# A GNN's first edge loop: two VectorE operands moved to PSUM, one-hots turned by TensorE, one score product instead of three, steps staggered

## Chip, cores, metric

One NeuronCore of a Trainium2 chip runs the whole program. The metric is the device time of one execution in microseconds (us), lower is better. The executions of one kernel are fast, that is, within 1.5% of the fastest execution of the same kernel in the same call. In the profile's lines PE is TensorE, PEld its loading of weights, DVE VectorE, ACT ScalarE and POOL GpSimd; SBUF and PSUM are the two on-chip memories in which the programs put the operands.

## The reference

Four layers work on N = 4096 nodes with D = 512 features and E = 65536 edges, sorted by destination. Only layer 0, a graph attention with H = 8 heads of F = 64, is concerned:

```python
def _L0_gnn_ref(x, edge_index, W, a):          # adj holds the edges and the diagonal
    h = jnp.einsum('nc,hcf->hnf', x, W)
    s_src = jnp.einsum('hnf,hf->hn', h, a[:, :F, 0])
    s_dst = jnp.einsum('hnf,hf->hn', h, a[:, F:, 0])
    e = s_src[:, :, None] + s_dst[:, None, :]
    e = jnp.where(e > 0, e, ALPHA * e)
    e = jnp.where(adj[None, :, :], e, NEG_INF)
    att = jax.nn.softmax(e, axis=-1)
    out = jnp.einsum('hij,hjf->hif', att, h)
    ...
x = x + _L0_gnn_ref(relu(layernorm(x)), edge_index, L0_gnn_W, L0_gnn_a)
# layers 1 to 3: other edge sums and dense products, unchanged by this case
```

## The kernel before

The edges are cut into tiles of 128, and eight tiles make a group; layer 0 has 68 groups. For each tile POOL issues one indirect gather: 128 rows of 2080 bytes, the node's 512 features and its eight score parts. The other part of a score belongs to the edge's own block of 128 nodes. It is fetched by a product of a turned one-hot matrix (`oh_t`, node by edge) with the block's node parts, which are kept as three bf16 pieces. VectorE weighs heads 0 to 5 of the rows, ScalarE heads 6 and 7; TensorE sums the rows into their nodes with the one-hot matrix (`oh`, edge by node); VectorE adds each pair's sum to `acc` ("keeps" it).

```python
def one_hots(pool, loc, t0, n):
    oh = pool.tile([P, n, P], F32, name="oh")
    nc.vector.tensor_tensor(oh, row_i.unsqueeze(1).to_broadcast([P, n, P]),          # L454
                            loc[:, t0:t0 + n].unsqueeze(2).to_broadcast([P, n, P]), op=OP.is_equal)
    return oh

# inside attend(): ep, eps are pools of two buffers (SBUF, PSUM)
def fetch(g):
    rows = ep.tile([P, GT, DA], F32, name="rows", bufs=4)
    for j in range(GT):
        gather(rows[:, j, :D + H], htab, s_dst[:, at(g) + j:at(g) + j + 1])          # L459, POOL
    return rows

def source_parts(g, places):          # places: the edges' node numbers, broadcast by a DMA
    oh_t = ep.tile([P, GT * P], BF16, name="oh_t")
    nc.vector.tensor_scalar(oh_t, places, col_i, None, op0=OP.is_equal)              # L703
    e_ps = eps.tile([P, GT, 2, H], F32, name="e_ps")
    ...                                # of[:, j // 2] = the block's three node parts, ScalarE
    for j in range(GT):
        for k in range(3):
            nc.tensor.matmul(e_ps[:, j]..., oh_t[:, j * P:(j + 1) * P],
                             of[:, j // 2, k, :], start=k == 0, stop=k == 2)         # L711
    return e_ps

def scores(rows, e_ps):
    u = ep.tile([P, GT, H], F32, name="u")
    nc.vector.tensor_add(u, e_ps[:, :, 0, :], rows[:, :, D:D + H])                   # L717
    ...                                # leaky relu, minus the bound, exp on ScalarE

def weights(g, rows, u):
    nc.vector.tensor_mul(rows[:, :, D:D + H], u, s_new[...]...)
    return one_hots(ep, s_loc, at(g), GT)

def weigh(j, rows):
    two = rows[:, j:j + 2]
    ...                                # heads 6 and 7 on ScalarE
    g = two[:, :, :VH * F].rearrange("p t (h f) -> p t h f", h=VH)
    nc.vector.tensor_mul(g, g, two[:, :, D:D + VH].unsqueeze(3).to_broadcast([P, 2, VH, F]))   # L739

# add_up: eight matmuls of a pair of tiles (L745); keep: acc += the pair's sum (L752)
for g in range(-3, groups):            # `if now(...)` guards cut
    rows[g + 3] = fetch(g + 3)
    places[g + 2] = fetch_places(g + 2)
    e_ps = source_parts(g + 1, places.pop(g + 1))
    ps = None
    for j in range(0, GT, 2):
        weigh(j, rows[g])
        if ps is not None:
            keep(g, j - 2, ps)
        ps = add_up(g, j, rows[g], done[g])
        if j == 2:
            u = scores(rows[g + 1], e_ps)
    done[g + 1] = weights(g + 1, rows[g + 1], u)
    keep(g, GT - 2, ps)
```

## Time and profile before

| | before |
|---|---|
| time, median of 4 runs (range) | 6489.0 us (6481.7 to 6496.5) |
| span of the profiled run | 6491.6 us |
| layer 0 edge loop, first gather to last keep | 277.9 to 1049.4 us: 771.5 us |
| distance of successive groups' scores, mean | 11.09 us |

The page's busy shares for the whole program do not speak of this loop: TensorE's come mostly from layer 2's dense products (2887 of its 5701 us lie between 2250 and 5230 us).

```profile
PE 5700.9 (88%) x18462; PEld 2779.8 (43%) x18462; DVE 4140.9 (64%) x7147; ACT 2940.7 (45%) x3977; POOL 3264.9 (50%) x3326
```

How to read the lines that follow in this document. A group of instructions has: line, engine, operation, tiles, shapes, count | busy us, mean ns of one | idle us just before them, and what ended it. A wait has: the engine, tile and line that waited, what released it, then us in all, number of waits, longest one. A timeline line has: start, duration, instruction, count, and in brackets the idle time before it. The loop itself is read in a stretch of steady state, as the prediction does.

### The profile page before, as it was taken

To read this page: it belongs to the slowest core of one execution; us is meant where nothing else is said; L and a number is where in the kernel's file an instruction comes from. 1 tells how busy PE (TensorE), PEld (TensorE's weight loads), DVE (VectorE), ACT (ScalarE), POOL (GpSimd) and SP (SyncE) were. 2 spreads that over 40 slices of the span, in tenths; PEclk is the share of its full clock that TensorE was granted. 3 is DMA by queue.
4 is the path that set the end of the run, shared out by engine and by line. 5 is a ranking of instruction groups with operands and counts; after the bars stand their busy time and mean duration, and the time that the engine had idled before them with its cause. 6 is when DMAs were issued, how large, how long until landed. Compare 5 with 4: busy or idle time off the path is not lost. (4 is left out here: it accounts for less than half of the span.)

```text
span 6491.6 us, 65768 instructions
## 1 busy us (share of the span) xinstructions
PE 5700.9 (88%) x18462; PEld 2779.8 (43%) x18462; DVE 4140.9 (64%) x7147; ACT 2940.7 (45%) x3977; POOL 3264.9 (50%) x3326
## 2 busy tenths in 40 slices
PE   6677787888779799999999999999999879978877
PEld 4366664322224344444444444444444456532222
DVE  7577778455534267766766766766776635556666
ACT  3244444300001277777777777777777633310000
POOL 1277772377760365555555555555555200017776
PEclk9899999999999899999999999999999999989999
DMA  8777775566774333333333333333333121127777
GB/s 226 181 215 219 216 218 172 164 201 201 195 215 177 130 115 100 98 105 101 99 102 103 99 100 105 99 98 106 100 99 104 52 81 62 62 93 209 222 243 221
DMA packets 400530, 926.42 MB, mean 143 GB/s; under 512 B 136695, under 2 KB 136695, under 8 KB 400151
## 3 DMA queue, kind: packets, MB, share of 16 engines
q0 software_dynamic: 230976, 721.66, 38.3%
q1 hardware_dynamic: 169174, 200.39, 9.8%
q8 instruction: 155, 2.54, 0.2%
q14 instruction: 225, 1.84, 0.1%
HBM read 818.71 MB, written 103.11 MB: 142 GB/s over the span
## 5 line engine op out<-in xcount | busy, mean ns | idle before, releaser
L448 PE MATMUL m_ps<-w_sb,h_t 128*128 128x512 f32 x4224 | 1906.0, 599 | 31.2 <-ACT h_t L969 31.2
L813 PE MATMUL sum_ps<-g,oh 128*128 128x512 f32 x2144 | 1133.7, 633 | 245.9 <-DMA g<-ztab,d_src 94.6
L448 PEld LDWEIGHTS m_ps<-w_sb,h_t 128*128 128x128 f32 x4224 | 771.2, 190 | 983.8 <-issue 791.3
L459 POOL DMA_INDIRECT qg<-qtab,eg x528 | 505.2, 957 | 990.2 <-ACT h_t L969 844.9
L459 POOL DMA_INDIRECT g<-ztab,d_src x528 | 514.0, 974 | 864.7 <-DMA x_end<-x 704.1
L469 DVE TENSOR_TENSOR acc<-acc,sum_ps 128x512 f32 x800 | 549.9, 687 | 543.8 <-PE sum_ps L813 517.4
L813 PEld LDWEIGHTS sum_ps<-g,oh 128*128 128x128 f32 x2144 | 340.7, 191 | 1026.6 <-DVE acc L469 356.5
L459 POOL DMA_INDIRECT g<-ytab,s_dst x544 | 535.5, 984 | 357.2 <-DMA ytab<-acc 187.9
L926 POOL DMA_INDIRECT eg<-aug,d_eid x528 | 568.9, 1077 | 244.1 <-issue 135.3
L459 POOL DMA_INDIRECT rows<-htab,s_dst x544 | 584.8, 1075 | 204.9 <-issue 139.3
L969 ACT COPY h_t<-tr_ps 128x512 f32<-128x512 f32 x528 | 283.7, 589 | 777.5 <-PE tr_ps L967 777.5
L745 PE MATMUL sum_ps<-rows,oh 128*128 128x261 f32 x2176 | 548.3, 408 | 62.1 <-PE sum_ps L745 37.0
L459 POOL DMA_INDIRECT pg<-ptab,eg x528 | 508.0, 962 | 160.9 <-issue 160.6
L745 PEld LDWEIGHTS sum_ps<-rows,oh 128*128 128x128 f32 x2176 | 425.4, 201 | 163.8 <-PE sum_ps L745 60.1
L979 PE MATMUL small_ps<-z,oh 128*128 128x512 f32 x1056 | 477.9, 595 | 8.4 <-DVE z L1039 8.4
L1018 DVE TENSOR_TENSOR z<-m_ps,b_bc 128x512 f32<-128x512 f32 x132 | 91.3, 692 | 467.4 <-PE m_ps L448 467.4
L469 DVE TENSOR_TENSOR acc<-acc,small_ps 128x512 f32 x528 | 360.8, 683 | 31.9 <-PE small_ps L979 4.4
L1192 ACT ACTIVATE t_end<-acc,dis 128x512 f32<-128x512 f32 x32 | 23.0, 721 | 663.7 <-DVE acc L469 663.7
L1004 DVE TENSOR_TENSOR z<-m_ps,b_bc 128x512 f32<-128x512 f32 x132 | 91.3, 692 | 352.9 <-PE m_ps L448 352.9
L1039 DVE TENSOR_TENSOR z<-z,t 128x1024 f32<-128x1024 f32 x264 | 310.3, 1217 | 8.2 <-ACTq L474 4.8
L979 PEld LDWEIGHTS small_ps<-z,oh 128*128 128x128 f32 x1056 | 201.5, 191 | 263.7 <-issue 221.9
L967 PEld LDWEIGHTS tr_ps<-ident,pg 128*128 128x128 f32 x2112 | 247.7, 141 | 150.8 <-issue 119.7
(252 smaller groups left out, 8389.0 us busy)
## 6 DMA issues: line engine op xcount, KB each, us to landing
aug<-row SPq DMA_DIRECT2D x32, 560.0 KB, 4.1
places<-loc_rows SPq DMA_DIRECT2D x68, 256.0 KB, 4.0
xt<-in_x_dram SPq DMA_DIRECT2D x16, 1024.0 KB, 6.5
row<-in_edge_attr_dram SPq DMA_DIRECT2D x32, 512.0 KB, 6.7
x<-xt SPq DMA_DIRECT2D x16, 1024.0 KB, 4.3
rows<-htab,s_dst POOLq DMA_INDIRECT x544, 3.9
g<-ytab,s_dst POOLq DMA_INDIRECT x544, 3.7
eg<-aug,d_eid POOLq DMA_INDIRECT x528, 2.7
```

Of the source, the lines that this page charges most:

```text
L448: nc.tensor.matmul(ps, h_t[:, k, :], w_sb[:, k0 + k, :], start=start and k == 0, stop=stop and k == KC - 1)
L459: nc.gpsimd.indirect_dma_start(out=dst_ap, out_offset=None, in_=table, in_offset=bass.IndirectOffsetOnAxis(ap=idx, axis=0))
L469: nc.vector.tensor_add(into, into, ps)
L745: nc.tensor.matmul(ps[:, c, :HW], oh[:, j + k, :], rows[:, j + k, c * HW:(c + 1) * HW], start=k == 0, stop=k == 1)
L813: nc.tensor.matmul(ps, oh[:, j + k, :], g[:, j + k, :], start=k == 0, stop=k == pair - 1)
L926: nc.gpsimd.indirect_dma_start(out=eg[:, j // 2, (j % 2) * HALF:(j % 2 + 1) * HALF], out_offset=None, in_=aug.rearrange("e c -> (e c)").un ...
L967: nc.tensor.transpose(h_ps[:, k, :], h[:, j, k * P:(k + 1) * P], ident)
L969: nc.scalar.copy(h_t, h_ps)
L979: nc.tensor.matmul(ps, oh, m, start=True, stop=True)
L1004: nc.vector.tensor_add(zz[:, 0, :], ps, b2_bc)
L1018: nc.vector.tensor_add(zz[:, 1, :], ps, b2_bc)
L1039: nc.vector.tensor_mul(mz[:, j:j + 2], mz[:, j:j + 2], t[:, j:j + 2])
```

## The change

Its intent: POOL's gathers take longer where they meet the weighing multiplies or the one-hots of the kernel before, VectorE instructions with two operands in SBUF (up to 1.73 us beside L739 and 1.95 beside L454, 0.947 in the median). So the weights that the multiply reads, and the node numbers that the one-hots compare with, go to PSUM. The room that this leaves is to be used by a shorter cycle of VectorE and TensorE: the turned one-hots come from TensorE and ScalarE instead of a VectorE compare of data that a DMA brings, the three parts of a score come from one product of 48 columns and are summed on VectorE, and the steps of neighbouring groups are interleaved. The core of the diff (removal of `loc_rows`, `col_i` and pieces that only change names are cut):

```diff
-    def one_hots(pool, loc, t0, n):
+    def one_hots(pool, loc, t0, n, bufs=None, ids=None):
-        nc.vector.tensor_tensor(oh, row_i.unsqueeze(1).to_broadcast([P, n, P]),
+        nc.vector.tensor_tensor(oh, (row_i if ids is None else ids).unsqueeze(1).to_broadcast([P, n, P]),
...
+            both_ps = kept.tile([P, P + 2 * GT * H], F32, name="both_ps")      # PSUM
+            ids_ps = both_ps[:, :P]
+            w_ps = both_ps[:, P:].rearrange("p (k t h) -> p k t h", k=2, t=GT)
+            nc.scalar.copy(ids_ps, row_i)
...
+            def turn(oh):                              # two t_ps tiles of four transposes each
+                        nc.tensor.transpose(t_ps[:, k, :], oh[:, j + k, :], ident)
-                nc.vector.tensor_scalar(oh_t, places, col_i, None, op0=OP.is_equal)
+                    nc.scalar.copy(oh_t[:, 4 * j:4 * j + 4, :], t_ps)
...
-                    for k in range(3):
-                        nc.tensor.matmul(e_ps[:, j]..., oh_t[:, j * P:(j + 1) * P],
-                                         of[:, j // 2, k, :], start=k == 0, stop=k == 2)
+                    nc.tensor.matmul(e_ps[:, j].rearrange("p k c -> p (k c)"), oh_t[:, j, :],
+                                     of[:, j // 2].rearrange("p k c -> p (k c)"), start=True, stop=True)
...
+                nc.vector.reduce_sum(near, e_ps.rearrange("p t k c -> p t c k"), axis=AX.X)
...
-                nc.vector.tensor_mul(rows[:, :, D:D + H], u, s_new...)
+                w = w_ps[:, g % 2]
+                nc.vector.tensor_mul(w, u, s_new...)
+                nc.scalar.copy(rows[:, :, D:D + H], w)
...
-                nc.vector.tensor_mul(g, g, two[:, :, D:D + VH].unsqueeze(3).to_broadcast([P, 2, VH, F]))
+                nc.vector.tensor_mul(part, part,
+                                     w_ps[:, g % 2, j:j + 2, :VH].unsqueeze(3).to_broadcast([P, 2, VH, F]))
...
+                rows[g + 3] = fetch(g + 3)             # the new order of a step, guards cut
+                made = turn(ohs[g + 1])
+                weigh(g, 0, rows[g]); sums[0] = add_up(g, 0, ...); weigh(g, 2, rows[g])
+                keep(g - 1, 6, sums.pop(6))
+                parts = turned(g + 1, made)
+                sums[2] = add_up(g, 2, ...); weigh(g, 4, rows[g]); keep(g, 0, sums.pop(0))
+                ohs[g + 2] = one_hots(ep, s_loc, at(g + 2), GT, 3, ids_ps)
+                e_ps = source_parts(*parts)
+                sums[4] = add_up(g, 4, ...)
+                u = scores(rows[g + 1], e_ps)
+                weigh(g, 6, rows[g]); keep(g, 2, sums.pop(2)); sums[6] = add_up(g, 6, ...)
+                weights(g + 1, rows[g + 1], u)
+                keep(g, 4, sums.pop(4))
```

More of the change, by code (lines that the diff above doesn't have):

```diff
@@ L88 @@
                    allow_small_or_imprecise_dtypes=True)
-    col_i = const.tile([P, 1], F32, name="col_i")
-    nc.gpsimd.iota(col_i, pattern=[[0, 1]], base=0, channel_multiplier=1,
-                   allow_small_or_imprecise_dtypes=True)
     acc = keep_pool.tile([P, NB, DA], F32, name="acc")
@@ L118 @@
     aug = dram.tile([E + 1, EA], F32, name="aug")
-    loc_rows = dram.tile([G * P, P], BF16, name="loc_rows")
     x1 = dram.tile([N, D], F32, name="x1")
@@ L315, in by_order @@
         placed(s_loc, loc)
-        low_p = pool.tile([P, G, P], BF16, name="low_p")
-        nc.vector.tensor_copy(low_p, loc)
-        nc.sync.dma_start(loc_rows.rearrange("(g p) c -> p g c", p=P), low_p)
         new = pool.tile([P, G, P], F32, name="new")
@@ L449, in product @@
                              start=start and k == 0, stop=stop and k == KC - 1)
-    def one_hots(pool, loc, t0, n):
-        oh = pool.tile([P, n, P], F32, name="oh")
-        nc.vector.tensor_tensor(oh, row_i.unsqueeze(1).to_broadcast([P, n, P]),
+    def one_hots(pool, loc, t0, n, bufs=None, ids=None):
+        oh = pool.tile([P, n, P], F32, name="oh", bufs=bufs)
+        nc.vector.tensor_tensor(oh, (row_i if ids is None else ids).unsqueeze(1).to_broadcast([P, n, P]),
                                 loc[:, t0:t0 + n].unsqueeze(2).to_broadcast([P, n, P]), op=OP.is_equal)
@@ L682, in run @@
             eps = ctx.enter_context(tc.tile_pool(name="edge_ps", bufs=2, space=PSUM))
+            kept = ctx.enter_context(tc.tile_pool(name="edge_keep", bufs=1, space=PSUM))
+            both_ps = kept.tile([P, P + 2 * GT * H], F32, name="both_ps")
+            ids_ps = both_ps[:, :P]
+            w_ps = both_ps[:, P:].rearrange("p (k t h) -> p k t h", k=2, t=GT)
+            nc.scalar.copy(ids_ps, row_i)
             groups = (last - first) // GT
@@ L693, in fetch, with turned @@
                 return rows
-            def fetch_places(g):
-                places = ep.tile([P, GT * P], BF16, name="places", bufs=3)
-                nc.sync.dma_start(places, loc_rows[at(g):at(g) + GT].rearrange("t c -> (t c)").partition_broadcast(P))
-                return places
-            def source_parts(g, places):
-                oh_t = ep.tile([P, GT * P], BF16, name="oh_t")
-                nc.vector.tensor_scalar(oh_t, places, col_i, None, op0=OP.is_equal)
-                e_ps = eps.tile([P, GT, 2, H], F32, name="e_ps")
+            def turn(oh):
+                made = []
+                for j in range(0, GT, 4):
+                    t_ps = eps.tile([P, 4, P], F32, name="t_ps")
+                    for k in range(4):
+                        nc.tensor.transpose(t_ps[:, k, :], oh[:, j + k, :], ident)
+                    made.append(t_ps)
+                return made
+            def turned(g, made):
+                oh_t = ep.tile([P, GT, P], BF16, name="oh_t")
+                for j, t_ps in enumerate(made):
+                    nc.scalar.copy(oh_t[:, 4 * j:4 * j + 4, :], t_ps)
                 of = ep.tile([P, GT // 2, 3, 2 * H], BF16, name="of")
@@ L708, in source_parts @@
                     nc.scalar.copy(of[:, j // 2], node3[:, ds(b, 1)].rearrange("p b k c -> p (b k) c"))
+                return oh_t, of
+            def source_parts(oh_t, of):
+                e_ps = eps.tile([P, GT, 3, 2 * H], F32, name="e_ps", bufs=1)
                 for j in range(GT):
-                    for k in range(3):
-                        nc.tensor.matmul(e_ps[:, j].rearrange("p c h -> p (c h)"), oh_t[:, j * P:(j + 1) * P],
-                                         of[:, j // 2, k, :], start=k == 0, stop=k == 2)
+                    nc.tensor.matmul(e_ps[:, j].rearrange("p k c -> p (k c)"), oh_t[:, j, :],
+                                     of[:, j // 2].rearrange("p k c -> p (k c)"), start=True, stop=True)
                 return e_ps
             def scores(rows, e_ps):
+                near = ep.tile([P, GT, 2 * H], F32, name="near")
+                nc.vector.reduce_sum(near, e_ps.rearrange("p t k c -> p t c k"), axis=AX.X)
                 u = ep.tile([P, GT, H], F32, name="u")
-                nc.vector.tensor_add(u, e_ps[:, :, 0, :], rows[:, :, D:D + H])
+                nc.vector.tensor_add(u, near[:, :, :H], rows[:, :, D:D + H])
                 nc.vector.scalar_tensor_tensor(u, u, 0.2, u, op0=OP.mult, op1=OP.max)
-                nc.vector.tensor_sub(u, u, e_ps[:, :, 1, :])
+                nc.vector.tensor_sub(u, u, near[:, :, H:])
                 nc.vector.tensor_scalar(u, u, SAFE_RANGE + 10.0, None, op0=OP.min)
@@ L726, in weights, with weigh_last @@
             def weights(g, rows, u):
-                nc.vector.tensor_mul(rows[:, :, D:D + H], u,
-                                     s_new[:, at(g):at(g) + GT].unsqueeze(2).to_broadcast([P, GT, H]))
-                return one_hots(ep, s_loc, at(g), GT)
-            def weigh(j, rows):
+                w = w_ps[:, g % 2]
+                nc.vector.tensor_mul(w, u, s_new[:, at(g):at(g) + GT].unsqueeze(2).to_broadcast([P, GT, H]))
+                nc.scalar.copy(rows[:, :, D:D + H], w)
+            def weigh_last(j, rows):
                 two = rows[:, j:j + 2]
@@ L737, in weigh @@
                                              scale=two[:, k, D + h:D + h + 1])
-                g = two[:, :, :VH * F].rearrange("p t (h f) -> p t h f", h=VH)
-                nc.vector.tensor_mul(g, g, two[:, :, D:D + VH].unsqueeze(3).to_broadcast([P, 2, VH, F]))
+            def weigh(g, j, rows):
+                part = rows[:, j:j + 2, :VH * F].rearrange("p t (h f) -> p t h f", h=VH)
+                nc.vector.tensor_mul(part, part,
+                                     w_ps[:, g % 2, j:j + 2, :VH].unsqueeze(3).to_broadcast([P, 2, VH, F]))
             def add_up(g, j, rows, oh):
@@ L752, in keep @@
                 nc.vector.tensor_add(into, into, ps[:, :, :HW])
-            rows, places, done = {}, {}, {}
-            for g in range(-3, groups):
+            rows, ohs, sums = {}, {}, {}
+            for g in range(-3, groups + 1):
                 now = lambda k: 0 <= k < groups
@@ L758, in run @@
                     rows[g + 3] = fetch(g + 3)
+                if now(g + 1):
+                    made = turn(ohs[g + 1])
+                if now(g):
+                    weigh(g, 0, rows[g])
+                    sums[0] = add_up(g, 0, rows[g], ohs[g])
+                    weigh_last(2, rows[g])
+                    weigh(g, 2, rows[g])
+                if now(g - 1):
+                    keep(g - 1, 6, sums.pop(6))
+                    del rows[g - 1], ohs[g - 1]
+                if now(g + 1):
+                    parts = turned(g + 1, made)
+                if now(g):
+                    sums[2] = add_up(g, 2, rows[g], ohs[g])
+                    weigh_last(4, rows[g])
+                    weigh(g, 4, rows[g])
+                    keep(g, 0, sums.pop(0))
                 if now(g + 2):
-                    places[g + 2] = fetch_places(g + 2)
+                    ohs[g + 2] = one_hots(ep, s_loc, at(g + 2), GT, 3, ids_ps)
                 if now(g + 1):
-                    e_ps = source_parts(g + 1, places.pop(g + 1))
-                ps = None
-                for j in range(0, GT, 2):
-                    if now(g):
-                        weigh(j, rows[g])
-                        if ps is not None:
-                            keep(g, j - 2, ps)
-                        ps = add_up(g, j, rows[g], done[g])
-                    if j == 2 and now(g + 1):
-                        u = scores(rows[g + 1], e_ps)
+                    e_ps = source_parts(*parts)
+                if now(g):
+                    sums[4] = add_up(g, 4, rows[g], ohs[g])
                 if now(g + 1):
-                    done[g + 1] = weights(g + 1, rows[g + 1], u)
+                    u = scores(rows[g + 1], e_ps)
                 if now(g):
-                    keep(g, GT - 2, ps)
-                    del rows[g], done[g]
+                    weigh_last(6, rows[g])
+                    weigh(g, 6, rows[g])
+                    keep(g, 2, sums.pop(2))
+                    sums[6] = add_up(g, 6, rows[g], ohs[g])
+                if now(g + 1):
+                    weights(g + 1, rows[g + 1], u)
+                    weigh_last(0, rows[g + 1])
+                if now(g):
+                    keep(g, 4, sums.pop(4))
         run()
```

## The prediction

> **What bounds the kernel now.** I read first the page, to find the stage, then one stretch of the steady edge loop of layer 0 (320 to 1000 us) as a table of busy times, as groups and as waits, then one group of eight tiles in order of time. The change touches this loop alone: its first gather starts at 277.9 us and its last sum is kept at 1049.4 us, 771 us of 6490, 12%. The stretch (columns: length, then busy us of PE, PEld, DVE, ACT, POOL, granted clock, DMA share, GB/s) and the page's row of the gathers:
>
> ```profile
> 320.00:1000.00 680.00, 540.39 (x3432) 424.41 (x3432) 532.09 (x921) 300.67 (x1342) 530.21 (x492) 0.95 0.77 217
> ```
>
> ```profile
> L459 POOL DMA_INDIRECT rows<-htab,s_dst x544 | 584.8, 1075 | 204.9 <-issue 139.3 <-ACT of L708 39.4 <-PE sum_ps L745 10.7
> ```
>
> PE, DVE and POOL each look busy for about 79%, so busy share names no bound. The gaps do. The waits of the stretch (us in total, times, longest):
>
> ```profile
> DVE acc L752 <- PE sum_ps L745: 136.9, 128, 3.0
> POOL rows L459 <- issue: 124.6, 409, 0.3
> ...
> PE e_ps L711 <- DVE oh_t L703: 85.9, 61, 1.5
> ...
> DVE u L717 <- DMA rows<-htab,s_dst: 3.7, 8, 0.8
> ```
>
> POOL's gaps are 0.30 us each and never longer, in front of every gather: that is the price of issuing, not a wait. 492 gathers of 1.079 us and their gaps fill 680 us, so **POOL never stands still**, and eight gathers set a pace of 11.07 us per group. The scores of successive groups start 11.11 us apart on average: the same. But VectorE and TensorE, waiting on each other (136.9 and 85.9 us above), are hardly faster. Undisturbed groups start 10.7 us apart; 24 of 67 take over 11.3 us, up to 12.4, and 23 of those meet one of the stretches of 3.4 us in which the granted clock is half, some 44 us apart (mean clock 0.95). So two loops of nearly equal length run side by side, and both must shrink for the stage to shrink.
>
> Why a gather takes 1.08 us when its median is 0.947 is seen where a group is laid out in time (start, us):
>
> ```profile
> 728.04 0.95 POOL L459 DMA_INDIRECT rows<-htab,s_dst  x1 [0.30 <-issue]
> 729.29 0.96 POOL L459 DMA_INDIRECT rows<-htab,s_dst  x1 [0.30 <-PE sum_ps L745]
> 730.56 1.62 POOL L459 DMA_INDIRECT rows<-htab,s_dst  x1 [0.30 <-issue]
> 732.49 0.95 POOL L459 DMA_INDIRECT rows<-htab,s_dst  x1 [0.30 <-issue]
> ```
>
> ```profile
> 729.97 0.54 DVE L703 TENSOR_SCALAR oh_t<-places,col_i 128x1024 bf16<-128x1024 bf16 x1
> 730.42 1.81 DVE L739 TENSOR_TENSOR rows<-rows 128x768 f32<-128x768 f32 x2
> 734.38 0.70 DVE L752 TENSOR_TENSOR acc<-acc,sum_ps 128x522 f32 x1 [2.14 <-PE sum_ps L745]
> ```
>
> The gather that meets the two weighing multiplies (L739, both inputs in SBUF) takes 1.62 us; those beside the sum from PSUM (L752) take 0.95. Counted over the loop, 135 of 544 gathers exceed 1.0 us, and the excess over 0.947 is 69 us, 62 us of it beside L739 and 7 beside the one-hots (L454) and L703.
>
> [...] The trace shows stretches of 3.4 us at 0.5, though TensorE never idles that long here (longest wait 1.7 us). In the next layer's loop, at 339 us busy of 400 (85%), the clock is 1.00. [...] at 512 elements an add from PSUM (L1150) takes 692 ns and one from SBUF (L1139) 685. So I charge nothing for moving an operand to PSUM.
>
> **The change part by part**, per group of eight tiles.
>
> *POOL.* The multiplies read their weights, and the one-hots their node numbers, from PSUM: one SBUF input each. The bf16 compare L703 goes. What remains with two SBUF inputs are short score steps (0.22 to 0.25 us each). The floor is 8 x (0.947 + 0.303) = 10.00 us; I allow 0.05 for the short steps: 10.05 against 11.07.
>
> *VectorE*, in intervals from start to start in the trace: four multiplies 4 x 0.87 = 3.48, four sums 4 x 0.61 = 2.44, one-hots 1.14, score steps 0.25 + 0.26 + 0.25 + 0.11 = 0.87, weight product 0.17. Removed: L703, 0.46. Added: the sum of a score's three parts, 384 elements; a reduction over 512 takes 0.668 us (L838), so 0.54, and 0.56 with the wait of the next step. Sum 8.7 us: not the bound.
>
> *TensorE.* The score products go from 24 matmuls to 8 of 48 columns, 0.76 to about 0.3 us. Added are eight transposes; layer 2 has them (eight in 1.04 us, one lasting 0.273, so 0.11 from start to start):
>
> ```profile
> 3000.45 1.04 PE L967 MATMUL tr_ps<-ident,pg 128*128 128x128 f32 x8
> ```
>
> Eight cost 0.87 us. Each of the four pair sums is eight matmuls 0.22 us apart, 1.76 us. Total 0.87 + 7.04 + 0.3 = 8.2 us.
>
> *ScalarE.* Added: two evictions of 128x512 (0.589 us each, L969) and one copy of weights (0.2). 300.67 / 61.3 = 4.9 us per group becomes 6.3: not the bound.
>
> *Order of steps.* The order of the changed program puts on TensorE: transposes for the next group, sum 0, sum 2, score products, sum 4, sum 6. Sum 6 waits for the multiply of tiles 6 and 7 and for a buffer that the keeping of sum 2 frees, and VectorE does both only after the scores. So one cycle goes: score products end, 0.17 of drain and 0.1 to VectorE; three-part sum 0.56; score steps 0.87; multiply 0.87; keep 0.70 and 0.1 back; sum 6 1.76; transposes 0.87; sums 0 and 2 3.52; score products 0.3. Sum: 0.27 + 0.56 + 0.87 + 0.87 + 0.80 + 1.76 + 0.87 + 3.52 + 0.3 = **9.82 us**, against 10.7 now. All else finishes earlier: ScalarE has the turned one-hots and node parts ready about 1.1 us before the products need them. TensorE waits 1.6 us per group instead of 2.3 ((680 - 540.39) / 61.3), [...] I charge 0.2 us per group for what is left, 10.0.
>
> *Sum.* Both loops land at about 10.05; with some jitter where they meet I take 10.12. 68 x (11.09 - 10.12) = 66 us. At the ends: the fill is unchanged, since first gather and landing are (278 to 291 us); the drain after the last gather loses perhaps 2 us, 22 to about 20 us. The reload of places through DMA (256 KB per group) goes, but it was hidden, as the gathers are bounded by their issue. No other stage changes. 6490 - 66 - 2 = **6422 us**.
>
> **The rivals.** (a) *The TensorE-VectorE cycle is the new bound.* If the strided three-part sum, the mixing of transposes with products or the half clock cost 0.7 us more than I have it, the pace is 10.6 and the gain 33 us: 6457. For it: its 9.82 is only 0.2 under POOL's floor, and every half-clock stretch lengthens it. Against: POOL runs some two groups ahead, which absorbs single long groups. (b) [...] gathers stay long[...]: pace 11, gain under 10 us, 6485. Against: short gathers sit exactly beside PSUM-reading work. (c) *ScalarE becomes late*: it now stands between transposes and products and between weights and the next multiply. If its loads of block numbers cost as much as in the first group (0.45 us idle each), 1.8 us are added to it and the 1.1 us of slack is gone: about 10.6, 6455. (d) *Everything fits*: 10.0 and a shorter drain, 6412.
>
> **Range and chances.** The floor of eight gathers allows 68 x 1.09 = 74 us at most, so with noise of the runs (6482 to 6496) less than 6405 is hardly possible; (a) and (c) reach 6457. The range is 6406 to 6454. A gain of over 2% is 130 us, which needs 9.2 us per group, under POOL's floor: 1%. A loss of 130 us needs 13 us per group, so a real serialisation: 2%. Within 2%: 97%.
>
> **What would show each step.** Gathers of the loop at mean 0.95 to 0.97 us, with no 1.6 us ones[...]; scores 10.0 to 10.2 us apart confirm the pace. If gathers are short but POOL shows gaps over 0.3 us, waiting for TensorE's last reading of a row buffer, then (a) or (c) holds, and the wait in front of sum 6 or of the score products tells which. Mean clock in the loop should rise above 0.95. The multiply from PSUM should stay at 0.95 us and the three-part sum at 0.54; each 0.1 us over on the latter lengthens the cycle by 0.1. A loop that ends before 970 us or after 1025 us makes the prediction wrong.

The sum: eight gathers at 10.00 and 0.05 for the short steps, 9.82 of the other cycle and 0.2 for the half-clock stretches that are left, so both at about 10.05, taken as 10.12; then 6490 - 66 - 2 = 6422 us. Moving an operand to PSUM is charged with nothing because of the two adds, 692 and 685 ns. Of the 0.27 us between products and three-part sum, 0.17 equals the length of one product in the trace of the kernel before (169 ns), and 0.1 what lies there between a multiply's end and the start of a sum that waited for it (0.10); that both are due in this place, and the 0.54 for the three-part sum, scaled down from 0.668, were estimates.

## The result, and the profile after

| | before | after |
|---|---|---|
| median of 4 runs (range), us | 6489.0 (6481.7 to 6496.5) | 6418.0 (6415.4 to 6427.3) |
| ratio, 95% interval | 1 | 0.9893 [0.9876, 0.9910] |
| span of the profiled run, us | 6491.6 | 6413.6 |
| edge loop, us | 771.5 | 696.2 |
| distance of scores, mean us | 11.09 | 10.01 |
| gather, mean us (of 544, those over 1.0 us) | 1.075 (135) | 0.946 (1) |

A ratio is the mean time of one kernel's fast runs over the mean of the other's of the same rounds, so it is not quite the ratio of the medians beside it. The change is a gain of 1.1%, inside the 2% that counts as "same". Of the 78.0 us between the two profiled runs, 75.4 are in this loop: 70.0 between its first and last gather and 5.4 in the drain behind the last one (21.3 us became 15.9). The loop starts 1.6 us later, and what follows it, which the change does not touch, is 4.3 us shorter. The medians differ by less, 71.0 us, since the profiled execution of the changed kernel is the fastest of its four.

The same stretch view of the changed kernel as the prediction opens with (length; busy us of PE, PEld, DVE, ACT, POOL; granted clock, DMA share, GB/s):

```profile
320.00:940.00 620.00, 529.43 (x2981) 437.77 (x2980) 545.02 (x931) 404.71 (x1552) 468.92 (x496) 0.99 0.77 214
```

The page's row of the gathers:

```profile
L451 POOL DMA_INDIRECT rows<-htab,s_dst x544 | 514.8, 946 | 209.2 <-issue 132.2
```

The 496 gathers of the stretch fill it: 496 x (0.946 + 0.303) = 619.5 of 620 us. So POOL again never stands still, at a pace of 10.0 us for eight. The waits of the stretch:

```profile
POOL rows L451 <- issue: 118.8, 390, 0.3
PE sum_ps L759 <- issue: 90.6, 62, 2.6
ACT of L711 <- issue: 84.3, 189, 0.7
DVE acc L766 <- PE sum_ps L759: 32.8, 61, 2.1
DVE u L726 <- DMA rows<-htab,s_dst: 6.5, 11, 1.3
```

POOL's gaps are still 0.3 us and never longer. VectorE's wait for sums has fallen from 136.9 to 32.8 us. TensorE has one wait per group left, 1.5 us on average in front of sum 6; the profile names no releaser for it ("issue"), and the timeline shows which it is. One group, from score products to score products:

```profile
702.62 0.36 PE L718 MATMUL e_ps<-of,oh_t 128*128 128x48 bf16 x8
...
703.02 0.56 DVE L724 TENSOR_REDUCE near<-e_ps 128x128 f32<-128x384 f32 x1
...
703.61 0.22 DVE L726 TENSOR_TENSOR u<-near,rows 128x64 f32<-128x64 f32 x1
...
704.50 0.95 DVE L752 TENSOR_TENSOR rows<-rows,both_ps 128x768 f32<-128x768 f32 x1
...
705.36 0.69 DVE L766 TENSOR_TENSOR acc<-acc,sum_ps 128x522 f32 x1
...
706.15 2.00 PE L759 MATMUL sum_ps<-rows,oh 128*128 128x261 f32 x8 [1.32 <-issue]
...
707.08 1.81 DVE L752 TENSOR_TENSOR rows<-rows,both_ps 128x768 f32<-128x768 f32 x2
...
707.31 0.94 POOL L451 DMA_INDIRECT rows<-htab,s_dst  x1 [0.30 <-issue]
...
707.99 1.03 PE L699 MATMUL t_ps<-ident,oh 128*128 128x128 f32 x8
...
708.56 0.95 POOL L451 DMA_INDIRECT rows<-htab,s_dst  x1 [0.30 <-issue]
...
708.87 3.69 PE L759 MATMUL sum_ps<-rows,oh 128*128 128x261 f32 x16
...
712.39 0.36 PE L718 MATMUL e_ps<-of,oh_t 128*128 128x48 bf16 x8
```

Sum 6 (706.15) starts 0.1 us after VectorE has kept sum 2 (705.36 + 0.69 = 706.05). And the gather of 707.31, which runs beside two weighing multiplies (707.08 to 708.89), takes 0.94 us; in the kernel before, the gather in that place took 1.62.

The multiply itself does not change its price with the operand's place, 951 ns before and 947 after, and neither do the one-hots (1216 ns in L454, 1218 in L446). The kernel before, by shape in its stretch:

```profile
L739 DVE TENSOR_TENSOR rows<-rows 128x768 f32<-128x768 f32 x246 | 229.2, 951 | 0.0
```

The changed kernel, with the added sum of three parts:

```profile
L752 DVE TENSOR_TENSOR rows<-rows,both_ps 128x768 f32<-128x768 f32 x249 | 230.8, 947 | 0.0
L724 DVE TENSOR_REDUCE near<-e_ps 128x128 f32<-128x384 f32 x62 | 34.6, 558 | 7.8
```

### The profile page after: what moved, and what is told of

Same layout as the page of the kernel before. It is cut to its first block, busy times and chain, and to the rows that moved or that the text cites. A ratio compares the mean times of both kernels' runs of the same rounds, so it can differ in the third digit from the quotient of the medians.

```text
span 6413.6 us, 64882 instructions
## 1 busy us (share of the span) xinstructions
PE 5686.2 (89%) x17918; PEld 2795.0 (44%) x17918; DVE 4147.7 (65%) x7146; ACT 3048.5 (48%) x4182; POOL 3185.6 (50%) x3325
## 5 line engine op out<-in xcount | busy, mean ns | idle before, releaser
L451 POOL DMA_INDIRECT g<-ztab,d_src x528 | 512.2, 970 | 866.7 <-DMA x_end<-x 706.1
L451 POOL DMA_INDIRECT g<-ytab,s_dst x544 | 530.6, 975 | 351.6 <-issue 292.5
L759 PE MATMUL sum_ps<-rows,oh 128*128 128x261 f32 x2176 | 528.6, 391 | 106.7 <-issue 98.8
L451 POOL DMA_INDIRECT rows<-htab,s_dst x544 | 514.8, 946 | 209.2 <-issue 132.2
L759 PEld LDWEIGHTS sum_ps<-rows,oh 128*128 128x128 f32 x2176 | 398.7, 191 | 189.2 <-issue 124.4
L1071 DVE TENSOR_TENSOR z<-z,t 128x1024 f32<-128x1024 f32 x264 | 310.2, 1216 | 8.2 <-ACTq L466 4.8
```

Of the source, the lines that this page charges most:

```text
L451: nc.gpsimd.indirect_dma_start(out=dst_ap, out_offset=None, in_=table, in_offset=bass.IndirectOffsetOnAxis(ap=idx, axis=0))
L759: nc.tensor.matmul(ps[:, c, :HW], oh[:, j + k, :], rows[:, j + k, c * HW:(c + 1) * HW], start=k == 0, stop=k == 1)
L1071: nc.vector.tensor_mul(mz[:, j:j + 2], mz[:, j:j + 2], t[:, j:j + 2])
```

## The experiments

The **theory** (A in the quoted expectations): two loops ran side by side in the kernel before, the gathers on POOL (11.07 us for eight) and the cycle of TensorE and VectorE (10.7 us where no stretch of half clock disturbs it). The operands in PSUM shorten the first, the order shortens the second, neither is worth anything alone, and in the changed kernel the eight gathers, at 10.0 us, are again what holds. The **rivals** (the other letters): one of the two parts brings it all (B the order, C the operands, by short gathers); the gain lies in the operations that were exchanged (turned one-hots, single product) instead of in operands and order; the changed kernel is held by its TensorE-VectorE cycle (9.8 us), not by POOL (D).

Four kernels came to a slow chip and were run again under new labels; the slow chips are told of at the end. Each result below is of a fast chip, beside runs of the kernel before on the same chip. All kernels gave correct results. "Excess" is the time of the 544 gathers over 0.947 us each; "POOL waits" is what its gaps exceed 0.305 us by.

| kernel | ratio to before [95%] | scores apart, us | gather mean, us | excess, us | POOL waits, us | loop, us |
|---|---|---|---|---|---|---|
| before | 1 | 11.09 | 1.075 | 70 | 0.1 | 771.5 |
| after | 0.9893 [0.9876, 0.9910] | 10.01 | 0.946 | 0.4 | 0.0 | 696.2 |
| w_sbuf_2: all but the weights in PSUM | 0.9996 [0.9979, 1.0013] | 11.11 | 1.082 | 73.5 | 0.1 | 769.2 |
| before_psum_2: operands alone | 1.0029 [1.0012, 1.0045] | 11.13 | 0.949 | 1.6 | 59 | 774.0 |
| scores_last_2 | 0.9894 [0.9877, 0.9910] | 10.02 | 0.948 | 0.7 | 0.1 | 695.8 |
| old_order_2 | 1.0399 [1.0382, 1.0416] | 14.90 | 0.950 | 2.6 | 300 | 1026.5 |
| three_products | 0.9887 [0.9871, 0.9904] | 10.02 | 0.948 | 0.7 | 0.0 | 696.9 |
| order_and_psum | 0.9887 [0.9870, 0.9903] | 10.03 | 0.950 | 2.3 | 0.0 | 697.6 |
| later_psum | 0.9853 [0.9836, 0.9869] | 10.01 | 0.946 | 0.3 | 0.0 | 695.9 |

### Order without the operand: the weights read from SBUF again

```diff
 # changed kernel, weigh()
-                                     w_ps[:, g % 2, j:j + 2, :VH].unsqueeze(3)...
+                                     rows[:, j:j + 2, D:D + VH].unsqueeze(3)...
```

> The changed kernel, but the weighing multiply on VectorE takes its weights from SBUF again (the copy that ScalarE makes), so it has two SBUF inputs; order of steps, transposes and all else stay. Theory A [...]: gathers of 1.6 us come back beside the pair of multiplies, 40 to 62 us of excess over 0.947 us in the loop, scores 10.6 to 10.9 us apart, 6455 to 6480 us. Rival B (the new order of steps alone made the gain, and the gathers grew shorter only with it): gathers stay at 0.95, pace 10.0, 6418 us within 6.

> The same kernel as w_sbuf, again, since on the chip of the first call even the kernel before took 7057 us instead of 6490, with unexplained stalls on several engines at once, so that no pace of this loop could be read there. Where the kernel before takes about 6490 us: theory A [...] expects gathers of 1.6 us back, 40 to 62 us of excess, pace 10.6 to 10.9 us and a ratio to the kernel before of 0.994 to 0.999; rival B (order alone) expects pace 10.0 and a ratio of 0.989. If this chip is again a slow one, neither is tested.

Measured: 6494.4 us (median of 4) beside 6499.3 of the kernel before, ratio 0.9996. This kernel keeps the new order, the new operations and the one-hots' operand in PSUM. The whole gain is gone, with one operand of one instruction moved. That is more than theory A had expected: excess of 73.5 us and not 40 to 62, scores 11.11 us apart and not 10.6 to 10.9, and a ratio just above its range of 0.994 to 0.999. Its gathers in the stretch 320 to 940 us, as a group:

```profile
L451 POOL DMA_INDIRECT rows<-htab,s_dst x447 | 485.0, 1085 | 136.2 <-issue 108.5 <-PE sum_ps L759 12.5 <-DMA rows<-htab,s_dst 5.8
```

And two successive gathers, with the multiply that the second one meets, in time:

```profile
603.28 0.95 POOL L451 DMA_INDIRECT rows<-htab,s_dst  x1 [0.30 <-issue]
...
604.37 0.95 DVE L752 TENSOR_TENSOR rows<-rows 128x768 f32<-128x768 f32 x1
604.53 1.61 POOL L451 DMA_INDIRECT rows<-htab,s_dst  x1 [0.30 <-issue]
```

The first gather ends before the multiply starts. The second begins while the multiply runs (604.37 to 605.32) and ends 0.82 us after the multiply's end (604.53 + 1.61 = 606.14). The whole loop shows the same: all 151 gathers over 1.0 us begin while such a multiply runs, and end 0.816 to 0.828 us after it. Of the 378 gathers that begin at another time none takes over 0.999 us, though 118 of them were still running when a multiply began. So a gather is lengthened if it begins during the multiply, and then ends about 0.82 us after it, whenever it began; one already under way is not lengthened. What holds the gather in between, no run shows. But it follows the operand's place: in the changed kernel, with the same multiplies at the same places of its order, 194 gathers begin while one runs, and the longest takes 0.955 us. Nor is it the row buffers, which multiply and gathers share: of the 135 long gathers of the kernel before, 113 began during L739, and 22 during the one-hots (L454), which touch no row buffer. They ended 0.813 to 0.823 us after either. The order is worth nothing while the gathers are long.

### Operands alone: the kernel before with PSUM operands

```diff
 # kernel before
+            ids_ps, w_ps = ...                 # PSUM tiles from a pool of their own
+            nc.scalar.copy(ids_ps, row_i)
...
-                nc.vector.tensor_mul(rows[:, :, D:D + H], u, s_new...)
-                return one_hots(ep, s_loc, at(g), GT)
+                w = w_ps[:, g % 2]
+                nc.vector.tensor_mul(w, u, s_new...)
+                nc.scalar.copy(rows[:, :, D:D + H], w)
+                return one_hots(ep, s_loc, at(g), GT, ids_ps)
...
-                nc.vector.tensor_mul(g, g, two[:, :, D:D + VH].unsqueeze(3)...)
+                nc.vector.tensor_mul(g, g, w_ps[:, g_ % 2, j:j + 2, :VH].unsqueeze(3)...)
```

> The kernel before, with only the operands moved: weights and node numbers read from PSUM, the weights copied back to the rows by ScalarE; products, places by DMA and order of steps as before. Theory A (two loops of nearly equal length lie side by side, and both must shrink): gathers fall to 0.95 us, but the TensorE-VectorE cycle stays at 10.7 us undisturbed and 11.0 to 11.1 on average, so 6475 to 6492 us; POOL gets real gaps, over 0.3 us, waiting for row buffers. Rival C [...]: pace 10.0 to 10.1, 6420 us.

> The same kernel as before_psum, again, for the same reason. Where the kernel before takes about 6490 us: theory A (two loops of nearly equal length) expects gathers at 0.95 us but the pace still 11.0 to 11.1, gaps of POOL over 0.3 us, and a ratio of 0.997 to 1.001; rival C [...] expects pace 10.0 to 10.1 and a ratio of 0.990.

Measured: 6516.6 us beside 6499.3, ratio 1.0029. The gathers of the stretch 320 to 940 us, as a group:

```profile
L459 POOL DMA_INDIRECT rows<-htab,s_dst x454 | 431.1, 950 | 189.2 <-issue 116.2 <-PE sum_ps L750 62.0 <-DMA rows<-htab,s_dst 7.6
```

The gathers are short (950 ns), but in place of the 70 us of excess stand 59 us in which POOL waits, mostly for TensorE's last reading of a row buffer. Scores are 11.13 us apart, nearly as before: the cycle of TensorE and VectorE holds. Pace and ratio lie just above what theory A had expected (11.0 to 11.1, 0.997 to 1.001). This kernel also has a step that the kernel before lacks, ScalarE's copy of the weights back to the rows. It does not explain the result: undisturbed groups follow each other at 10.76 us, against 10.70 in the kernel before. Together with w_sbuf_2 this settles the main question. The change without the weights in PSUM gives 0.0%, the operands in PSUM without the rest -0.3%, both together 1.1%: two loops of nearly equal length side by side, and each hid the gain in the other. The rivals that gave one part the whole gain fall. (What the one-hots' operand is worth by itself was not tried in this loop; later_psum below tries it in two others.)

### What holds the changed kernel now: three versions with a shorter cycle

If eight gathers are the floor, then a shorter TensorE-VectorE cycle gains nothing. The first try moved the scores behind the last multiply:

```diff
 # changed kernel, end of a step
-                    u = scores(rows[g + 1], e_ps)
                     weigh_last(6, rows[g]); weigh(g, 6, rows[g])
                     keep(g, 2, sums.pop(2)); sums[6] = add_up(g, 6, rows[g], ohs[g])
+                    u = scores(rows[g + 1], e_ps)
```

> The changed kernel with the multiply of tiles 6 and 7, the keeping of sum 2 and sum 6 ahead of the scores of the next group, so that sum 6 no longer waits for the scores: the TensorE-VectorE cycle loses its 1.3 us of waiting and falls to about 9 us. Theory A (eight gathers of 0.947 + 0.303 us are the floor that the changed kernel has reached): pace 10.00, 6414 us within 6, VectorE waits more for rows by DMA. Rival D (the TensorE-VectorE cycle, at 9.77 us undisturbed and 10.01 on average, is the bound and POOL merely keeps up): pace 9.2 to 9.5, 6365 to 6385 us.

> The same kernel as scores_last, again, for a chip on which the kernel before takes about 6490 us. The two runs before this have shown that either half of the change alone gives nothing. This asks which loop bounds the changed kernel (pace 10.01). Theory A (eight gathers, 10.00 us, are its floor): with the TensorE-VectorE cycle cut by its 1.3 us of waiting the pace stays at 10.00, the long groups (over 10.5 us) go, VectorE waits more for rows by DMA, ratio to the kernel before 0.987 to 0.990. Rival D (the TensorE-VectorE cycle is the bound): pace 9.2 to 9.5, ratio 0.981 to 0.984.

Measured: 6422.5 us beside 6492.4, ratio 0.9894, the time of the changed kernel, as the theory has it. But the reasoning of this expectation failed. VectorE does not wait more for gathered rows, but 2.1 us in the stretch 320 to 940 us, against 6.5 in the changed kernel, and 4 of 67 groups still take over 10.5 us (8 before this edit). How long the cycle is can be read where the program lags behind the gathers after a half-clock stretch and catches up: there groups follow each other at 9.74 us (once at 9.26), not at about 9. The wait had only moved, from sum 6 to sum 0 of the next step, which now waits for exp, weights, their copy and the first multiply. A cycle of 9.74 instead of 9.77 us tells nothing about the floor, so this run does not separate theory and rival.

The next two take the exchanged operations out, one after the other. `three_products` has the old product, three accumulating matmuls a tile, and no sum on VectorE:

```diff
-                e_ps = eps.tile([P, GT, 3, 2 * H], F32, name="e_ps", bufs=1)
+                e_ps = eps.tile([P, GT, 2 * H], F32, name="e_ps", bufs=1)
...
+                    for k in range(3):
+                        nc.tensor.matmul(e_ps[:, j], oh_t[:, j, :], of[:, j // 2, k, :], start=k == 0, stop=k == 2)
...
-                nc.vector.reduce_sum(near, e_ps.rearrange("p t k c -> p t c k"), axis=AX.X)
+                near = e_ps
```

> The changed kernel with the three parts of a score as three accumulating products again (24 matmuls, 0.76 us) in place of one product and a sum on VectorE (0.36 us on TensorE, 0.59 on VectorE). By the cycle of the prediction this adds 0.4 us on TensorE and takes 0.59 on VectorE, both in the same chain: 9.77 becomes about 9.6 us. Theory A: POOL's floor hides it, pace 10.00 to 10.03, ratio within 0.001 of the changed kernel's 0.989. Rival (this part carries a share of the gain): pace 10.3 or more, ratio 0.992 or more.

Measured: 6420.6 us beside 6492.4, ratio 0.9887; scores 10.02 us apart; catching up it does 9.56. In its waits of the stretch 320 to 940 us:

```profile
DVE u L725 <- DMA rows<-htab,s_dst: 33.9, 30, 2.8
```

In the changed kernel the same wait was 6.5 us: what the shorter cycle saves is spent waiting for gathered rows.

`order_and_psum` also drops the transposes and takes the turned one-hots from the DMA's `places` with a VectorE compare, as the kernel before did. What is left of the change is order and operands:

```diff
 # three_products, and further
-                    made = turn(ohs[g + 1])
+                    places[g + 2] = fetch_places(g + 2)
...
-                for j, t_ps in enumerate(made):
-                    nc.scalar.copy(oh_t[:, 4 * j:4 * j + 4, :], t_ps)
+                nc.vector.tensor_scalar(oh_t.rearrange("p t c -> p (t c)"), places, col_i, None, op0=OP.is_equal)
```

> The changed kernel without its transposes and without the one product: the turned one-hots come again from places by DMA and VectorE's compare, a score's three parts are again three accumulating products; only the operands in PSUM and the new order of steps stay. By the cycle of the prediction TensorE loses 0.87 us of transposes and gains 0.4, VectorE gains 0.46 of compare and loses 0.59, so the cycle is under 9.5 us. Theory A (operands and order are all that the gain needs): gathers 0.95 to 0.96 us (a little excess beside the compare), pace 10.0 to 10.1, ratio 0.989 to 0.991. Rival (the turning by TensorE carries a share[...]): pace 10.4 or more, ratio 0.993 or more. If the kernel before does not take about 6490 us here, neither is tested.

Measured: 6415.7 us beside 6488.2, ratio 0.9887; scores 10.03 us apart, though catching up it does 8.90. The gathers of the stretch, and VectorE's wait for them:

```profile
L458 POOL DMA_INDIRECT rows<-htab,s_dst x495 | 470.1, 950 | 150.8 <-issue 124.9 <-PE sum_ps L759 12.8 <-DVE u L730 5.5
```

```profile
DVE u L726 <- DMA rows<-htab,s_dst: 40.4, 22, 3.2
```

A cycle of 8.90 us and one of 9.77 give the same pace and the same time. So the floor is POOL's eight gathers, and the rival that put the TensorE-VectorE cycle first falls. It also follows that the single product and the turning by TensorE carry no share of the gain that these runs can resolve: without both, the ratio is 0.9887 against 0.9893. (The bf16 compare came back with `places`: 15 gathers are over 1.0 us, 11 of which begin during it, with 2.3 us of excess in all. The half-clock stretches came back too, 13 in the loop at a mean clock of 0.95. Neither shows in the time.)

### The new operations in the old order

```diff
 # changed kernel; in turned(): the node parts copied before the two evictions; the step:
+                    e_ps = source_parts(*turned(g + 1, turn(ohs[g + 1])))
+                for j in range(0, GT, 2):
+                    weigh_last(j, rows[g]); weigh(g, j, rows[g])
+                    if ps is not None:
+                        keep(g, j - 2, ps)
+                    ps = add_up(g, j, rows[g], ohs[g])
+                    if j == 2:
+                        u = scores(rows[g + 1], e_ps)
+                ohs[g + 2] = one_hots(ep, s_loc, at(g + 2), GT, 3, ids_ps)
+                weights(g + 1, rows[g + 1], u)
+                keep(g, GT - 2, ps)
```

> The changed kernel with all its new operations, but the steps in the order of before (transposes, eviction and score products at the start of a step, scores after the second multiply, weights at the end). Theory A: gathers at 0.95 us, but TensorE waits for ScalarE's eviction between transposes and products (1.2 us) and VectorE's three-part sum lies in front of the third sum (0.6 us), so a pace of 11.0 to 11.6 us and 6485 to 6525 us, with gaps of POOL over 0.3 us. Rival C ([...] order does not matter while POOL sets the pace): 6418 us within 8.

> The same kernel as old_order, again, for the same reason. Theory A: gathers at 0.95 us, pace 11.0 to 11.6 us, gaps of POOL over 0.3 us, ratio 0.999 to 1.006: the transposes, the eviction and the three-part sum cost more than they bring unless the steps are staggered. Rival: the new operations by themselves shorten the cycle, pace 10.0 to 10.5, ratio 0.989 to 0.994.

Measured: 6748.6 us beside 6492.4, ratio 1.0399, scores 14.90 us apart. The direction was expected, the size missed by far: 11.0 to 11.6 us had been expected. Its stretch and one group:

```profile
320.00:940.00 620.00, 449.55 (x1996) 343.70 (x1995) 367.97 (x621) 261.23 (x1038) 320.47 (x338) 0.86 0.53 146
```

```profile
712.46 1.09 PE L699 MATMUL t_ps<-ident,oh 128*128 128x128 f32 x8 [0.17 <-DVE oh L446]
...
715.44 0.23 ACT L709 COPY of<-node 128x48 bf16 x1 [0.43 <-issue]
715.58 1.06 ACT L711 CAST oh_t<-t_ps 128x512 bf16<-128x512 f32 x2
...
716.21 0.27 PE L718 MATMUL e_ps<-of,oh_t 128*128 128x48 bf16 x4 [2.66 <-ACT oh_t L711]
```

TensorE turns the one-hots and then stands for 2.66 us, because ScalarE first copies four node parts, 0.23 us each and an idle 0.43 to 0.44 us in front of each, where the program loads the block number into a register, and then evicts. With these waits comes a lower clock (0.86 in the stretch, 57 half-clock stretches in the loop), and a product of the sums takes 454 ns on average in place of 391 in the changed kernel. So the transposes, which cost nothing where the order puts other sums between them and the products (10.01 us apart with them, 10.03 without them and the single product), come with 3.8 us a group more than the kernel before where it does not (14.90 - 11.09). How much of this is the wait itself and how much the clock, no run separates. The order was needed for the new operations to be free, and the expectation left out that ScalarE's chain stands between them.

### The same cure for layers 1 and 3

Their edge loops also build one-hots from two SBUF operands. One PSUM copy of the node numbers goes there too:

```diff
 # changed kernel, sum_edges()
+                ids_ps = bps.tile([P, P], F32, name="ids_ps")
+                nc.scalar.copy(ids_ps, row_i)
...
-                        ohs[i + 1] = one_hots(ep, loc, first + (i + 1) * U, U)
+                        ohs[i + 1] = one_hots(ep, loc, first + (i + 1) * U, U, None, ids_ps)
```

> The changed kernel, and in the edge loops of layers 1 and 3 too the one-hots read their node numbers from PSUM. Those loops were bounded by POOL as well: gathers of 0.975 and 0.970 us with gaps of 0.30, 16 and 13 us of excess, of which some 13 and 12 us lie beside the one-hots. Theory A: gathers there fall to 0.95 to 0.955 us, 15 to 25 us less than the changed kernel, ratio to the kernel before 0.985 to 0.987. Rival: the excess there comes from the sort's min and max steps and the final adds, or is taken up by other waits: under 6 us, ratio 0.988 to 0.990.

Measured: 6393.6 us (6390.7 to 6403.5) beside 6492.4, ratio 0.9853. Gathers of the changed kernel in those loops, then of this one (groups of the whole run):

```profile
L451 POOL DMA_INDIRECT g<-ytab,s_dst x544 | 530.6, 975 | 351.6 <-issue 292.5 <-DMA g<-ytab,s_dst 30.3 <-PE sum_ps L845 28.2
L451 POOL DMA_INDIRECT g<-ztab,d_src x528 | 512.2, 970 | 866.7 <-DMA x_end<-x 706.1 <-issue 122.2 <-PE sum_ps L845 20.4
```

```profile
L451 POOL DMA_INDIRECT g<-ytab,s_dst x544 | 516.6, 950 | 352.8 <-issue 295.7 <-PE sum_ps L847 28.5 <-DMA g<-ytab,s_dst 28.3
L451 POOL DMA_INDIRECT g<-ztab,d_src x528 | 502.5, 952 | 868.1 <-DMA x_end<-x 707.5 <-issue 125.2 <-PE sum_ps L847 18.6
```

The gathers lose 530.6 - 516.6 = 14.0 and 512.2 - 502.5 = 9.7 us; the loops lose 14.4 (707.8 to 693.4) and 9.6 (672.7 to 663.1). The loops shrink by what their gathers shrink, so nothing else holds them, and the gain arrives in full without any reordering. This version is the fastest. It was not timed in the same call as the changed kernel itself, but the two versions of that call that equal it in time, scores_last_2 and three_products, took 6422.5 and 6420.6 us, 27 to 29 us more. Equal code differs a little here: in their profiled executions the two loops took 711.5 and 673.1 us, and 711.8 and 676.0, so that against them later_psum's two loops are 28 to 31 us shorter.

### Slow chips

> The kernel of order_and_psum (operands in PSUM and staggered steps, no transposes, no one product) with the one-hots of layers 1 and 3 reading their node numbers from PSUM as in later_psum. If the effects add, as the theory of three loops each at POOL's floor wants: gathers of all three loops at 0.946 to 0.955 us, ratio to the kernel before 0.984 to 0.987, the same as later_psum. If the gain of later_psum had come with its new first loop, or chip to chip, it would be 0.988 to 0.990.

`simple_best` joins `order_and_psum` and `later_psum`. It and the four kernels met chips on which everything was slower. Each of these two chips was met in one call only, so the chip and its state at that moment cannot be told apart. On one the kernel before took 7057 us (median of 7), on another 7087 (median of 11), 9% more than on the others. There all variants lost to it:

| kernel, slow chip | median, us | before | ratio [95%] |
|---|---|---|---|
| w_sbuf | 7213.7 | 7057.2 | 1.0229 [1.0201, 1.0257] |
| before_psum | 7288.1 | 7057.2 | 1.0334 [1.0314, 1.0354] |
| old_order | 7251.2 | 7057.2 | 1.0271 [1.0253, 1.0289] |
| scores_last | 7124.5 | 7057.2 | 1.0093 [1.0076, 1.0110] |
| simple_best (another chip) | 7351.4 | 7086.6 | 1.0368 [1.0345, 1.0390] |

The traces of these runs show short gathers where the operands are in PSUM (0.948 to 0.952 us), but POOL waiting 257 to 432 us for row buffers, and layers 1 and 3 slow as well (787 to 807 us in layer 1's loop in place of about 708). Several engines stop at once without a wait that the profile explains. Two lines of scores_last on the slow chip:

```profile
304.31 0.23 ACT L711 COPY of<-node 128x48 bf16 x1 [4.57 <-issue]
...
316.92 0.70 DVE L766 TENSOR_TENSOR acc<-acc,sum_ps 128x522 f32 x1 [12.96 <-remote]
```

VectorE keeps a sum 7.7 us after TensorE has finished it, and ScalarE's idle time in front of the copy of a node part, 0.4 us elsewhere, is 4.6. The packets of the gathers' DMA queue take no longer there (median 161 ns in this loop on both kinds of chip). What makes these chips slow is open: no profile of the kernel before was taken there (its executions list a granted clock of 0.91 to 0.92 in place of 0.97), and the changed kernel never ran there. The expectations had been formed from fast chips, so these five runs test none of the theories. Whether the gains of `order_and_psum` and `later_psum` add up stays untried, too. But one warning stands: a gain of 1% measured on one set of chips turned into a loss of 0.9% on another for scores_last, a version that equals the changed kernel on a fast chip.

## Why the prediction was right

Predicted 6422 us, measured 6418; the sign, the size and the cause were as predicted. That the two numbers meet so closely is in part luck: in the profiled executions the loop gained 75.4 us where the prediction had 66 + 2, while its start came 1.6 later. Of its own pictures, rival (d) fits the traces best: a pace of 10.0 us and a shorter drain, for which it had 6412; the measured time lies between. By its own steps:

- **POOL bounds the loop, and its gathers are long where they meet the multiply or the one-hots with two SBUF inputs.** Shown: w_sbuf_2 brings the long gathers back with one operand, and the changed kernel has 0.4 us of excess where the kernel before had 70. Rival (b), that the gathers stay long, falls. One detail was misread: the compare L703, named among those that lengthen gathers, began none of the 135 long ones (113 began during L739, 22 during L454). The allowance of 0.05 us per group for the short score steps, which still read two SBUF operands, was not needed: 0.4 us in 68 groups is 0.006 each.
- **TensorE and VectorE form a second loop, so both must shrink.** Shown by w_sbuf_2 and before_psum_2, neither of which is faster than the kernel before. (The distance of scores in the kernel before is 11.09 us by its trace, as in the prediction's sum, and not 11.11.)
- **The cycle of 9.82 us.** The timeline above gives 9.77 (702.62 to 712.39), term by term:

| term | predicted, us | timeline |
|---|---|---|
| score products and hand-over | 0.57 | 703.02 - 702.62 = 0.40 |
| three-part sum | 0.56 | 0.59 |
| score steps | 0.87 | 0.89 |
| multiply | 0.87 | 0.86 |
| keep and way back | 0.80 | 0.79 |
| sum 6 | 1.76 | 1.84 |
| transposes | 0.87 | 0.88 |
| sums 0 and 2 | 3.52 | 3.52 |

  The one term clearly mis-sized is the first: it charged the products (0.3) and then 0.27 after them, while in the timeline they take 0.36 and the sum starts 0.04 after their end. Rival (a), this cycle as the new bound, falls by three_products and order_and_psum.
- **Busy times per group**: POOL's floor 10.00, measured pace 10.01. TensorE 8.54 us (predicted 8.2), VectorE 8.79 (8.7), ScalarE 6.53 (6.3), from the stretch of 62 groups: each somewhat over, none the bound. (The prediction's first two are distances from start to start, so they compare only roughly with busy time.)
- **The half clock.** The prediction charged 0.2 us per group to the cycle. In fact 3 stretches are left in 620 us, where there were 19 in 680, and the clock is 0.99. The outcome was right. A link to TensorE's shorter waits is not shown: order_and_psum waits as little (95 us in the same 620, the changed kernel 91) and has 12 stretches. What sets them off is open. (Those of the kernel before follow each other after 10 to 55 us, 34 in the median, and not after some 44.)
- **The pace.** 10.12 was POOL's 10.00, 0.05 for the short score steps and 0.07 for jitter where the two loops meet. Neither allowance was needed: the pace was 10.01. From first to last gather the loop gained 70.0 us, not 66.
- **The drain** behind the last gather gained 5.4 us, not 2. The loop started 1.6 later.
- **ScalarE.** Rival (c) was half right: an idle time of about 0.45 us stands in front of three of a group's four node parts, where the block numbers are loaded (84.3 us in all, 189 times, the ACT wait above), and the slack in front of the products is 0.4 us, not 1.1: the last node part is copied by 711.96, the products start at 712.39. It did not bind, but old_order_2 shows what it does when the order gives it no room.

Measured in medians the gain is 71 us against a predicted 68. The loop ended at 975.7 us, inside the 970 to 1025 that the prediction had set as its test. What the prediction did not ask, and the runs answered: two of the four parts of the change, the single product and the turned one-hots, were not needed for the gain.

## What to carry to other kernels

When two engines' loops have nearly the same length, no single cure shows in the time (here 0.0% and -0.3% alone, 1.1% together); look for both before judging either, and test each alone. A long VectorE instruction (0.95 and 1.22 us) with two SBUF inputs beside a stream of indirect gathers was paid for by the gathers here (70 us of excess in the loop, 0.4 after), and one operand moved to PSUM took that away at no cost to the instruction (951 ns before, 947 after); where the gathers were the only bound, as in layers 1 and 3, that one line brought its whole gain (14.4 and 9.6 us). Transposes and evictions were free here (scores 10.01 us apart) only where the order put other work between them and their consumer; in the old order they were 14.90 apart. And a gain of 1% has to be looked at on more than one chip.
